# Attention with a gated feed-forward: earlier value sums, split operands for two more score steps, one split moved by a step

## The chip, the core and the metric

The kernel runs on one core of a Trainium2 chip. The core has a matrix engine (TensorE, PE in the profile; its weight loads are listed apart as PEld), VectorE (DVE), ScalarE (ACT), GpSimd (POOL) and SyncE (SP), which here does nothing but start DMA transfers. Each engine works off its own list of instructions in order, and waits where an instruction needs something that another engine or a transfer has not finished. The metric is the device time of one execution in microseconds: 544.22 us before the change, the median of three runs (544.18 to 544.31).

## The reference

The input `x` has the shape (2, 1024, 512): two sequences of 1024 tokens. What is computed, cut to its core:

```python
xn = layernorm(x)
q, k, v = (xn @ W.T + b for W, b in ((Wq, bq), (Wk, bk), (Wv, bv)))      # 32 heads of 16
att = softmax(where(causal, q @ k.T / 4, -inf));  s = (att @ v) @ Wo.T + bo
logits = xn @ W_gate.T;  w = top-2 of softmax(logits), normalized       # 8 experts of rank 16
ffn = xn @ W_base.T + b_base + sum_e w_e * (xn @ A_e.T) @ B_e.T
out = x + s * silu(ffn)
```

Everything is float32.

## The kernel before

**Units and steps.** The tokens of a sequence are cut into two chunks of 512 (`c` = 0, 1), and the 32 heads into four groups of eight (`oc`). Attention runs over 16 units `(b, oc, c)`, in the order of the list `units` (line 1387, pairs swapped at 1391): (0,0,0), (0,1,0), (0,0,1), (0,1,1), (0,2,0), (0,3,0), (0,2,1), and so on. A unit of the first chunk has 5 steps, one of the second 13; `plan` (line 1393) numbers all 144 steps. A step `n` makes the transposed scores of a stretch of keys for four pairs of heads (`scores`, line 1691), their exponentials on ScalarE, a causal mask on GpSimd (`masked`), and, one step later, the product with the values (`values`, line 1738).

**Score operands.** Heads lie in pairs within strips of 32 partitions, and a matmul takes one head of each pair (`par`). The first unit uses whole float32 operands: `qT` holds the queries twice, each time with the other head of the pair multiplied by zero (`queries(par)`, line 392), and the keys `kT` (tile kf_0_0_0) are used as they are. All later units use split operands: rounded (fp32r) values in one half of a strip and the remainder that rounding left in the other. The remainder is made by VectorE (`split_queries`, `split_keys`), the queries' copy of it by ScalarE (`copy_remainder`), and it is put into the other half of the strip by DMAs from SBUF to SBUF on SP's queue (`place_queries`, `place_keys`, two transfers each). The first unit's keys are split too, by `apart` (line 438), since the third unit, (0,0,1), attends to them; it runs at step 4 or later.

**The plan of the other work.** The order of all instructions on every engine is written out by the program itself. After each step, `fill(n)` (line 1592) places other work in this order: TensorE tasks (projections, feed-forward) as far as a share of the total and the due times ask for; splits that are due; the list `later`; zero-cost tasks such as `layernorm_task`, which have VectorE work and DMAs. An entry of `later` is a step and a function; it runs in the first `fill` that is not before the step, unless `costs` names a limit until which it may wait for ScalarE to be calm. What is placed first stays first on its engine and, for DMAs, on SP's queue. `fill(-2)` comes ahead of step 0 and holds all of `first_task` (line 362): layernorm, transposes and first projections of chunk (0,0).

**Around the change.** In `fill(0)` `early_values` (line 832) makes the first values by a scheme of seven block products instead of eight; for it VectorE first takes differences of the weights (t1 to t4, tiles wt1 to wt4) and of the tokens (s0 to s3, tiles asum). Its products p1, p2, p6, p7, p4 use two PSUM buffers in turn (`ps_mm`, `bufs=2`), so p6 starts when p1 has been added into `v`, and p4 when p6 has. p1, p2 and the first quarter of p6 stand in `fill(0)`, the rest of p6, p7 and the first quarter of p4 in `fill(1)`, the rest of p4 and the whole `qk_task` of the second unit in `fill(2)`. `layernorm_task(0, 1)` takes its statistics (four `bn_stats`) in `fill(0)`, and in `fill(1)` it normalizes, transposes half of the chunk into `sq` and calls:

```python
            if not b:
                store()
                place()
```

`store` writes `sq` to a DRAM scratch (scr<-sq), and `place` reads it back in four transfers (xnT<-scr), the first of which must wait until the write has landed. `room` counts free buffers; a task starts only when its `takes` are free. `ve` and `act` are wrappers that add up estimated time for the planner; `nc.vector` is the same engine without that.

Of the kernel before, what the change touches and what calls it, by code (L numbers as in the profile page):

```python
# [18 lines left out]
P = 128  # L19
# [12 lines left out]
NEG = -3.0e38  # L32
NF = 2 + 4 * 2 * 4
WARM = 10


Z_LOW, Z_HIGH = 1.0e-20, 1.0e20
# [60 lines left out]
def direct(ctx, tc, sound, x, wq, wk, wv, wo, wb, wa, wg, wB, bq, bk, bv, bo, bb, out):  # L98
# [148 lines left out]
    WAIT = object()  # L247
    PAUSE = object()
    turned_at, now = {}, [0]
    xns, xnTs, kTs, qTs, vs, gs, oTs, kfs = {}, {}, {}, {}, {}, {}, {}, []  # L250

    def mm_tile(name):
        return ps_mm.tile([P, D], F32, tag="mm", name=name)
# [108 lines left out]
    def first_task():  # L362

        xnT = sb.tile([P, KC, C], F32, tag="xnT", bufs=3, name="xnT_0_0")
        qT = sb.tile([P, 2, C], F32, tag="qT", bufs=2, name="qT_0_0_0")
        kT = sb.tile([P, C], F32, tag="kf", bufs=2, name="kf_0_0_0")
        xnTs[0, 0], qTs[0, 0, 0] = xnT, qT
        kfs.append(kT)
        pq = ps_av.tile([P, C], F32, tag="av", name="pq_first")
        pk = ps_av.tile([P, C], F32, tag="av", name="pk_first")  # L370

        def turn(t):
            many = KC if t else KC // 2
            for k0 in range(0, KC, many):
                pt = mm_tile("pt_x")[:, 0 : many * P]
                for k in range(many):
                    cols = slice((k0 + k) * P, (k0 + k + 1) * P)
                    nc.tensor.transpose(pt[:, k * P : (k + 1) * P], first[t][:, cols], ident)
                act.copy(
                    xnT[:, k0 : k0 + many, t * P : (t + 1) * P],  # L380
                    pt.rearrange("p (k t) -> p k t", k=many),
                )
            turned_at[0, 0] = now[0] - 5

        def project_first(ps, w, t):
            cols = slice(t * P, (t + 1) * P)
            for k in range(KC):
                nc.tensor.matmul(  # L388
                    ps[:, cols], lhsT=w[:, k, :], rhs=xnT[:, k, cols], start=k == 0, stop=k == KC - 1
                )  # L390

        def queries(par):
            ve.tensor_scalar(
                qT[:, par], pq, bq_sb[:, 0:1], half[:, par : par + 1], ALU.add, ALU.mult
            )

        def keys(t0, t1):
            cols = slice(t0 * P, t1 * P)
            act.activation(kT[:, cols], pk[:, cols], AF.Identity, bias=bk_sb[:, 0:1])

        s0 = yield from statistics(first[0 : 1])

        def halves():
            for half_ in range(2):
                normalize([first[0][:, 2 * P * half_ : 2 * P * (half_ + 1)]], *s0)

        s1 = yield from statistics(first[1:2], between=halves)
        turn(0)
        normalize(first[1:2], *s1)
        project_first(pq, wqks[0][:, 2 * KC : 3 * KC], 0)  # L410
        b_ps = mm_tile("b_ps")[:, 0 : 2 * KC]
        nc.tensor.transpose(b_ps, b_rows, ident[0 : 2 * KC, 0 : 2 * KC])
        act.copy(b_sb, b_ps)
        s2 = yield from statistics(first[2 : 3])
        turn(1)
        project_first(pk, wqks[0][:, 3 * KC :], 0)
        keys(0, 1)
        project_first(pq, wqks[0][:, 2 * KC : 3 * KC], 1)
        normalize(first[2:3], *s2)
        turn(2)  # L420
        s3 = yield from statistics(first[3 : 4])
        project_first(pk, wqks[0][:, 3 * KC :], 1)
        project_first(pq, wqks[0][:, 2 * KC : 3 * KC], 2)
        normalize(first[3:4], *s3)
        turn(3)
        room["x"] += 1
        project_first(pk, wqks[0][:, 3 * KC :], 2)
        project_first(pq, wqks[0][:, 2 * KC : 3 * KC], TT - 1)
        queries(0)
        queries(1)  # L430
        ve.stream_shuffle(b_pair, b_sb, PAIRED)
        ve.tensor_tensor(b_less, b_pair[:, 0:KC], b_pair[:, KC:], ALU.subtract)
        project_first(pk, wqks[0][:, 3 * KC :], 3)
        keys(1, TT)
        kTs[0, 0, 0] = sb.tile([P, 2, C], F32R, tag="kT", bufs=4, name="kT_0_0_0")
        low = sb.tile([P, C], F32, tag="rb", bufs=1, name="low_0_0_0")

        def apart():
            ve.stream_shuffle(low, kT, PAIRED)
            split_keys(kTs[0, 0, 0], low, low)  # L440
            later.append((now[0] + 1, lambda: place_keys(kTs[0, 0, 0], low)))

        later.append((0, lambda: pair_up(wqks[1])))
        paired = lambda: pair_up(wqks[0])
        costs[paired], costs[apart] = (1.1, 5), (1.1, 6)
        later.append((3, paired))
        later.append((4, apart))
        yield 8 * MM

    def qk_task(b, oc, c):  # L450
# [47 lines left out]
    def split_keys(kT, kf, low):  # L498

        act.activation(kT, kf.unsqueeze(1).to_broadcast([P, 2, C]), AF.Copy)  # L500
        ve.tensor_tensor(low, kf, kT[:, 0].bitcast(F32), ALU.subtract)

    def place_keys(kT, low):
        for par in range(2):
            sp.dma_start(out=kT[1 - par :: 2, par].bitcast(F32), in_=low[par::2])
# [17 lines left out]
            both = qT[:, 2 * par : 2 * par + 2].bitcast(F32)  # L523
            sp.dma_start(out=both[1 - par :: 2], in_=both[par::2])

    def last_unit(unit):
        return 1 if unit == units[-1] else 0

    def split(b, oc, c, qf, kf):

        qT, kT = split_tiles(b, oc, c)
        split_keys(kT, kf, kf)

        def queries():
            split_queries(qT, qf)
            room["acc"] += 1
            later.append((now[0] + 1, remainder))

        def remainder():
            copy_remainder(qT)  # L540
            urgent.append((now[0], lambda: place_queries(qT)))

        by = starts[b, oc, c] - last_unit((b, oc, c))
        costs[queries], costs[remainder] = (1.1, by - 4), (0.6, by - 3)
        later.append((now[0] + 1, queries))
        urgent.append((now[0] + 1, lambda: place_keys(kT, kf)))
# [282 lines left out]

    def early_values():

        x0 = xnTs[0, 0]
        at = lambda i, j: x0[:, 2 * j : 2 * j + 2, BK * i : BK * i + BK]
        early_at["w"] = raw = {
            (i, j): wv_sb[:, 2 * i : 2 * i + 2, BK * j : BK * j + BK]
            for i in range(2) for j in range(2)
        }
        t = {  # L840
            n: sb.tile([P, 2, BK], F32, tag="wp", bufs=NWP, name=f"wt{n}") for n in range(1, 5)
        }
        early_sums.update({f"t{n}": t[n] for n in t})
        early_at["s"] = s = [
            sb.tile([P, 2, BK], F32, tag=f"sum{n}", bufs=1, name=f"asum{n}") for n in range(4)
        ]
        vt = value_tile(0, 0)
        for i in range(TT):
            vs[0, i] = vt[:, i]
        hv = heads(vt)  # L850
        early_at["v"] = slot = lambda i, j: hv[:, 2 * i : 2 * i + 2, H // 2 * j : H // 2 * (j + 1), 0:HD]
        s11, s12, s21, s22 = slot(0, 0), slot(0, 1), slot(1, 0), slot(1, 1)
        ve.tensor_tensor(t[1], raw[0, 1], raw[0, 0], ALU.subtract)
        ve.tensor_tensor(s[2], at(0, 0), at(1, 0), ALU.subtract)
        ve.tensor_tensor(s[1], at(1, 1), s[2], ALU.subtract)
        ve.tensor_tensor(t[2], raw[1, 1], t[1], ALU.subtract)
        ve.tensor_tensor(t[3], raw[1, 1], raw[0, 1], ALU.subtract)
        p1 = yield from early_product("p1", at(0, 0), raw[0, 0])
        early_add(s12, p1, early_bias(0))
        ve.tensor_tensor(t[4], raw[1, 0], t[2], ALU.subtract)  # L860
# [607 lines left out]
    for b in range(NB):  # L1468
        for c in range(NC):
            s0 = starts[b, 0, c]  # L1470
            xn = [("xnT", b, c)]
            if not b and not c:
                room["x"] -= 1
                Task(1, first_task(), 8 * MM, takes={"xnT": 1, "qT": 1, "kT": 1}, uses=xn)
            else:
                Task(
                    s0 - (12 if c else 25) if b else -9, layernorm_task(b, c), 0.0, after=s0 - (44 if c == 0 else 30) if b else -9,
                    takes={"x": 1, "xnT": 1}, frees={"x": 1},
                )
# [112 lines left out]
    def fill(n):  # L1592
# [52 lines left out]
        enough = lambda more=0.65: late_by(n + 1, begins, more) > 0  # L1645
        calm = lambda more: act.free + more < begins + 0.75
        for x in [x for x in splits if x[0] <= n]:
            if room["qT"] and room["kT"] and (calm(1.1) or n >= starts[x[2]] - 5 - last_unit(x[2])):
                splits.remove(x)
                room["qT"] -= 1  # L1650
                room["kT"] -= 1
                x[1]()
# [38 lines left out]
    def scores(n):  # L1691
# [1 line left out]
        place_urgent(n)  # L1693
        ss = [ps_s.tile([P, 2, C], F32, tag="s", name=f"s{p}") for p in range(2)]
        for m, (par, kt, q0, w, col) in enumerate(pieces):
            first_unit = (b, oc, c) == units[0]
            halves = 1 if first_unit else 2
            keys = kfs[0] if first_unit else kTs[b, oc, kt // TT][:, par]
            q = qTs[b, oc, c]
            for half_ in range(halves):  # L1700
                for s in range(4):
                    rows = slice(32 * s, 32 * s + 32)


                    nc.tensor.matmul(  # L1705
                        ss[s // 2][:, s % 2, col : col + w],
                        lhsT=keys[rows, kt % TT * P : kt % TT * P + P],
                        rhs=q[rows, halves * par + half_, q0 : q0 + w],
                        start=m + half_ == 0,
                        stop=m == len(pieces) - 1 and half_ == halves - 1,  # L1710
                    )
# [572 lines left out]
```

## Time and profile before

| | us |
|---|---|
| median of the runs | 544.22 |
| the profiled execution | 544.11 |
| its span on the core | 542.3 |

Busy time of the engines in the stretches around the change, in us, from the profile:

| stretch (us) | what runs | PE | DVE | ACT | POOL |
|---|---|---|---|---|---|
| 0 to 16 | `first_task` | 14.40 | 7.40 | 4.43 | 3.12 |
| 16 to 21 | step 0, p1, p2 | 4.67 | 4.93 | 3.48 | 1.98 |
| 21 to 27 | step 1, p6, p7 | 5.90 | 5.52 | 2.05 | 1.74 |
| 27 to 33 | step 2, p4, queries of unit 2 | 6.00 | 5.97 | 2.02 | 1.80 |
| 33 to 39 | keys of unit 2, step 3 | 6.00 | 1.64 | 3.76 | 0.00 |
| 39 to 46 | steps 3 to 5 | 7.00 | 3.98 | 5.37 | 2.80 |
| 100 to 500 | most of the rest | 399.84 | 256.34 | 280.85 | 88.23 |

A row is read as the time in which the engine had an instruction at work within the stretch; what is missing to its length is idle time. TensorE is at work nearly all the time, the other engines about half of it, except for VectorE between 16 and 33 us.

### The profile page before, as it was taken

What the parts mean: (1) busy time and instruction counts of PE and PEld (TensorE: products, weight loads), DVE (VectorE), ACT (ScalarE), POOL (GpSimd) and SP (SyncE); (2) the same over time, 40 slices, a digit from 0 to 9 for tenths busy, and PEclk for the clock granted to TensorE, in tenths of its full rate; (3) what the DMA queues carried; (4) which work ended last, traced back from release to release, by engine and by line L of the source; (5) the groups of instructions that cost most, each with busy time, mean ns of one, the idle gap of its engine ahead of it and who ended that gap; (6) DMA issues with size and microseconds to landing.
All of it is one profiled execution on the core that took longest, in us unless ns stands there. A gap on an engine that the chain in (4) does not pass through costs nothing.

```text
span 542.3 us, 19668 instructions
## 1 busy us (share of the span) xinstructions
PE 532.7 (98%) x8503; PEld 280.4 (52%) x8503; DVE 340.5 (63%) x703; ACT 352.2 (65%) x390; POOL 117.0 (22%) x249
## 2 busy tenths in 40 slices
PE   8999999999999999999999999999999999999994
PEld 8546445544455554454545554454545554456661
DVE  4863586665584976566369766574176554749833
ACT  3457755777776876757667756657667776877641
POOL 2213401021033422030133321130113330121300
PEclk9999999999999999999999999999999999999998
DMA  7636356366527583813656545640134121752301
GB/s 253 157 118 201 126 171 221 95 201 203 160 100 231 186 257 123 225 42 105 196 155 199 190 131 174 199 142 24 63 98 142 61 85 46 234 176 85 100 29 59
DMA packets 67743, 78.13 MB, mean 144 GB/s; under 512 B 9928, under 2 KB 52944, under 8 KB 67136
## 3 DMA queue, kind: packets, MB, share of 16 engines
q1 hardware_dynamic: 67632, 76.78, 44.9%
q8 instruction: 69, 1.13, 0.9%
q14 instruction: 26, 0.21, 0.1%
q10 hardware_dynamic: 16, 0.00, 0.0%
HBM read 45.34 MB, written 19.37 MB: 119 GB/s over the span
## 4 chain that ended last, share of the span: by engine, by line
PE 95%; DVE 2%; ACT 1%; DMA 1%; issue 0%; SPq 0%; POOL 0%; ACTq 0%; POOLq 0%; DVEq 0%
PE av L1757 26%; PE p L258 25%; PE s L1705 18%; PE q L258 14%; PE ph L258 3%; PE po L258 2%; PE pq L258 1%; PE pk L258 1%; PE warm L213 1%; ACT pt L56 1%; PE pq_first L388 1%; PE h L258 1%; DMA kept<-w_gate 1%; PE pk_first L388 0%; DVE wt L56 0%; PE pt_o L258 0%
## 5 line engine op out<-in xcount | busy, mean ns | idle before, releaser
L56 ACT ACTIVATE pt<-s 128x1024 f32<-128x1024 f32 x288 | 290.6, 1025 | 150.8 <-PE s L1705 145.4
L1733 POOL TENSOR_SCALAR_AFFINE_SELECT pt<-pt 128x256 f32<-128x256 f32 (+1 forms) x224 | 108.3, 498 | 399.3 <-ACT pt L56 398.7
L1757 PE MATMUL av<-pt,v 128*32 128x512 f32 (+3 forms) x1680 | 154.4, 467 | 0.2 <-DVE oT L56 0.2
L1705 PE MATMUL s<-qT,kT 32*128 32x512 f32 (+3 forms) x1616 | 107.4, 363 | 0.1
L1705 PEld LDWEIGHTS s<-qT,kT 32*128 32x128 f32 x1616 | 61.5, 183 | 57.8 <-issue 34.0
L1757 PEld LDWEIGHTS av<-pt,v 128*32 128x32 f32 x1680 | 41.1, 108 | 53.5 <-issue 38.4
L258 PE MATMUL p<-wt,asum 128*32 128x256 f32 x960 | 58.4, 379 | 0.4 <-DVE v L56 0.4
L258 PE MATMUL q<-asum,wqk 128*32 128x256 f32 x832 | 51.1, 379 | 0.0
L258 PEld LDWEIGHTS p<-wt,asum 128*32 128x32 f32 x960 | 31.0, 110 | 29.9 <-issue 12.6
L258 PE MATMUL q<-xnT,wqk 128*32 128x256 f32 x624 | 39.5, 379 | 0.0
L258 PEld LDWEIGHTS q<-asum,wqk 128*32 128x32 f32 x832 | 26.8, 110 | 23.8 <-issue 6.6
L258 PEld LDWEIGHTS q<-xnT,wqk 128*32 128x32 f32 x624 | 20.2, 110 | 18.5 <-issue 6.6
L56 DVE SCALAR_TENSOR_TENSOR kf<-q,kf 128x256 f32<-128x256 f32 x39 | 16.5, 422 | 20.6 <-PE q L258 20.0
L56 DVE TENSOR_TENSOR g<-p,g 128x512 f32<-128x512 f32 x20 | 13.8, 689 | 23.5 <-PE p L258 23.4
L258 PE MATMUL p<-w,xnT 128*32 128x256 f32 x448 | 27.6, 379 | 0.0
L56 DVE TENSOR_TENSOR v<-p,v 128x512 f32<-128x512 f32 x22 | 15.0, 684 | 13.4 <-PE p L258 13.3
L258 PE MATMUL p<-w,asum 128*32 128x256 f32 x320 | 21.0, 379 | 0.0
L258 PEld LDWEIGHTS p<-w,xnT 128*32 128x32 f32 x448 | 14.9, 110 | 10.6 <-issue 3.3
L258 PEld LDWEIGHTS ph<-wag_sb,xnT 128*32 128x32 f32 x512 | 15.2, 110 | 3.9 <-issue 3.0
L56 DVE TENSOR_TENSOR x<-p,x 128x512 f32<-128x512 f32 x15 | 10.3, 685 | 10.4 <-PE p L258 10.4
L258 PE MATMUL ph<-wag_sb,xnT 128*32 128x136 f32 x512 | 16.6, 279 | 0.0
L56 ACT ACTIVATE qT<-qf 128x1024 fp32r<-128x1024 f32 x15 | 15.8, 1054 | 0.1
(153 smaller groups left out, 562.2 us busy)
## 6 DMA issues: line engine op xcount, KB each, us to landing
wt<-kept SPq DMA_DIRECT2D x36, 256.0 KB
qT<-qT SPq DMA_DIRECT2D x30, 256.0 KB
x<-in_x_dram SPq DMA_DIRECT2D x16, 256.0 KB
kept<-wqk SPq DMA_DIRECT2D x16, 256.0 KB
wqk<-kept SPq DMA_DIRECT2D x4, 1024.0 KB
kT<-kf SPq DMA_DIRECT2D x30, 128.0 KB
scr<-sq SPq DMA_DIRECT2D x6, 512.0 KB
xnT<-scr SPq DMA_DIRECT2D x24, 128.0 KB
```

Source lines behind the costliest of these rows:

```text
L56: return getattr(self.engine, name)(*args, **named)
L213: nc.tensor.matmul(warm[:, n % 4 * P : n % 4 * P + P], lhsT=ident, rhs=ident, start=True, stop=True)
L258: nc.tensor.matmul(o[j : j + 32], lhsT=lhsT[:, j : j + 32] if len(lhsT.shape) == 2 else lhsT[:, j // 32], rhs=rhs, start=start, stop=stop,)
L388: nc.tensor.matmul(ps[:, cols], lhsT=w[:, k, :], rhs=xnT[:, k, cols], start=k == 0, stop=k == KC - 1)
L1705: nc.tensor.matmul(ss[s // 2][:, s % 2, col : col + w], lhsT=keys[rows, kt % TT * P : kt % TT * P + P], rhs=q[rows, halves * par + half_, ...
L1733: nc.gpsimd.affine_select(out=d, in_=d, compare_op=ALU.is_ge, fill=0.0, base=0, pattern=[[0, d.shape[1]], [1, P]], channel_multiplier=-1,)
L1757: nc.tensor.matmul(avs_now[par][32 * s : 32 * s + 32, q0 : q0 + w], lhsT=vs[b, kt][:, h * VS - HD * par : h * VS - HD * par + HP], rhs=pt[ ...
```

## The change

- **Sums ahead.** `early_begin` is new. It takes four of the five differences that stood at the head of `early_values` (t1, t2, t3 and s2) and issues them inside `first_task`, ahead of `queries(0)`, through `nc.vector`. s1 stays where it was.
- **Split operands from step 3.** The whole `qT` and `kT` serve steps 0 to 2 only (`SPLIT_FROM = 3`). ScalarE makes the first unit's queries once more, as they are (`qf`). `apart` moves from step 4 or later to `fill(0)` without a condition; it now also shuffles and splits the queries. `remainder` and the two key transfers follow in `fill(1)`, the two query transfers in `fill(2)`, which is the last place ahead of the scores of step 3. The first task takes two `qT` buffers, and gives one back in `fill(2)`.
- **Seventh unit.** `last_unit` becomes `sooner`, and holds for (0,2,1) as well: its split may be forced at 6 instead of 5 steps ahead of its start, and the limits for its queries and its remainder come one step sooner.

```diff
+SPLIT_FROM = 3
...
-        xnTs[0, 0], qTs[0, 0, 0] = xnT, qT
-        kfs.append(kT)
+        xnTs[0, 0] = xnT
+        whole_first.extend((qT, kT))
...
         project_first(pk, wqks[0][:, 3 * KC :], 2)
+        early_begin()
         project_first(pq, wqks[0][:, 2 * KC : 3 * KC], TT - 1)
         queries(0)
         queries(1)
+        qf = sb.tile([P, C], F32, tag="qf", bufs=2, name="qf_0_0_0")
+        act.activation(qf, pq, AF.Identity, bias=bq_sb[:, 0:1])
...
         keys(1, TT)
-        kTs[0, 0, 0] = sb.tile([P, 2, C], F32R, tag="kT", bufs=4, name="kT_0_0_0")
+        q2, k2 = split_tiles(0, 0, 0)
         low = sb.tile([P, C], F32, tag="rb", bufs=1, name="low_0_0_0")
+        turns.append((SPLIT_FROM - 1, lambda: room.update(qT=room["qT"] + 1)))
 
         def apart():
+            qs = sb.tile([P, C], F32, tag="qf", bufs=2, name="qs_0_0_0")
             ve.stream_shuffle(low, kT, PAIRED)
-            split_keys(kTs[0, 0, 0], low, low)
-            later.append((now[0] + 1, lambda: place_keys(kTs[0, 0, 0], low)))
+            ve.stream_shuffle(qs, qf, PAIRED)
+            split_keys(k2, low, low)
+            split_queries(q2, qs)
+            later.append((now[0] + 1, lambda: place_keys(k2, low)))
+            later.append((now[0] + 1, remainder))
+
+        def remainder():
+            copy_remainder(q2)
+            later.append((now[0] + 1, lambda: place_queries(q2)))
 
         later.append((0, lambda: pair_up(wqks[1])))
         paired = lambda: pair_up(wqks[0])
-        costs[paired], costs[apart] = (1.1, 5), (1.1, 6)
+        costs[paired] = 1.1, 5
+        later.append((0, apart))
         later.append((3, paired))
-        later.append((4, apart))
...
-    def last_unit(unit):
-        return 1 if unit == units[-1] else 0
+    def sooner(unit):
+        return 1 if unit in (units[6], units[-1]) else 0
...
+    def early_begin():
...
+        nc.vector.tensor_tensor(t[1], raw[0, 1], raw[0, 0], ALU.subtract)
+        nc.vector.tensor_tensor(t[2], raw[1, 1], t[1], ALU.subtract)
+        nc.vector.tensor_tensor(t[3], raw[1, 1], raw[0, 1], ALU.subtract)
+        nc.vector.tensor_tensor(s[2], at(0, 0), at(1, 0), ALU.subtract)
+
+    def early_values():
...
-        ve.tensor_tensor(t[1], raw[0, 1], raw[0, 0], ALU.subtract)
-        ve.tensor_tensor(s[2], at(0, 0), at(1, 0), ALU.subtract)
         ve.tensor_tensor(s[1], at(1, 1), s[2], ALU.subtract)
-        ve.tensor_tensor(t[2], raw[1, 1], t[1], ALU.subtract)
-        ve.tensor_tensor(t[3], raw[1, 1], raw[0, 1], ALU.subtract)
...
-                Task(1, first_task(), 8 * MM, takes={"xnT": 1, "qT": 1, "kT": 1}, uses=xn)
+                Task(1, first_task(), 8 * MM, takes={"xnT": 1, "qT": 2, "kT": 1}, uses=xn)
...
-            if room["qT"] and room["kT"] and (calm(1.1) or n >= starts[x[2]] - 5 - last_unit(x[2])):
+            if room["qT"] and room["kT"] and (calm(1.1) or n >= starts[x[2]] - 5 - sooner(x[2])):
...
-            first_unit = (b, oc, c) == units[0]
-            halves = 1 if first_unit else 2
-            keys = kfs[0] if first_unit else kTs[b, oc, kt // TT][:, par]
-            q = qTs[b, oc, c]
+            whole = n < SPLIT_FROM
+            halves = 1 if whole else 2
+            keys = whole_first[1] if whole else kTs[b, oc, kt // TT][:, par]
+            q = whole_first[0] if whole else qTs[b, oc, c]
```

The tiles and slices that `early_begin` sets up (`at`, `raw`, `t`, `s`) moved into it with the four instructions, and `early_values` reads them from `early_at`.

## The prediction

> **What bounds the kernel.** I read the page's busy shares first, then its chain of waits.
>
> ```profile
> PE 532.7 (98%) x8503; PEld 280.4 (52%) x8503; DVE 340.5 (63%) x703; ACT 352.2 (65%) x390; POOL 117.0 (22%) x249
> PE 95%; DVE 2%; ACT 1%; DMA 1%; issue 0%; SPq 0%; POOL 0%; ACTq 0%; POOLq 0%; DVEq 0%
> ```
>
> TensorE is busy for 98% and carries 95% of the chain that ends last. By stretches, it misses 0.16 us between 100 and 500 us. So there is no slack after the start in which a delay could vanish: a microsecond in which TensorE stands still early is a microsecond at the end, and only less TensorE work or a closed gap gains. Next, the chain from 15 to 38 us:
>
> ```profile
> 15.08 1.47 DVE qT L56 x2
> ...
> 18.73 1.71 DVE wt L56 x2
> 20.44 0.61 DVE v L56
> 21.05 0.04 issue
> 21.10 0.64 PE p L258 x8
> ...
> 34.08 3.43 PE pk L258 x32
> 37.51 1.08 PE s L1705 x16
> ```
>
> Here VectorE bounds: its differences (`wt`, `asum`) hold up the addition of p1, and p6 waits for that addition's buffer. From 21.1 on TensorE runs unbroken up to step 3 (37.51). VectorE and SP around it, by the timeline:
>
> ```profile
> 22.16 0.41 DVE L56 TENSOR_TENSOR bv_sb<-bv_sb 128x256 f32<-128x256 f32 x1
> 22.50 0.68 DVE L56 BATCH_NORM_STATS2 st<-x 128x6 f32<-128x512 f32 x1
> ...
> 25.89 0.69 DVE L56 TENSOR_TENSOR v<-p,v 128x512 f32<-128x512 f32 x1
> ...
> 30.16 1.41 DVE L56 STREAM_TRANSPOSE sq<-x 128x256 f32<-128x256 f32 x4
> ```
>
> ```profile
> 26.63 0.16 PEld L258 LDWEIGHTS p<-wt,xnT 128*32 128x32 f32 x8 [0.29 <-DVE v L56]
> ```
>
> ```profile
> 31.60 0.33 SPq L72 DMA_DIRECT2D scr<-sq  x1
> 34.90 2.65 SPq L72 DMA_DIRECT2D xnT<-scr  x4
> 37.65 1.21 SPq L72 DMA_DIRECT2D qT<-qT  x2
> ```
>
> The reader should see two tight couplings. The addition of p6 (25.89) comes only after the four `bn_stats`, and p4 already waits for it (26.63). And SP stands still from 31.93 to 34.90 until scr<-sq has landed; what is behind xnT<-scr stands too.
>
> **Sums ahead.** Four instructions, 0.60 us from start to start (wt 16.89, asum 17.49 in the chain), go into VectorE's gap between 12.05 and 15.08, when it waits for pq_first. s2 needs the copy of the fourth tile (ACT, ends 13.75), so the four end near 14.6; cost nothing. If wv landed late the first queries would slip: 0 to 0.9 us (all of that load's traffic is over by 13.5), and I take 0. p1 can then be added at 18.9 instead of 20.36, and p6 follows p2 without the gap: chain time of p1 and p2 is 3.47 (as for the 64 matmuls at 23.80), 17.01 + 3.47 = 20.48 against 21.10, so 0.6 us gained up to there. p2's addition is bound by p2 itself (20.67), so VectorE reaches its `bn_stats` place at about 21.67 instead of 22.50.
>
> **Steps 3 and 4.** Whole: 1.08 and 1.07 us to the values (37.44 to 38.52, 41.25 to 42.32). Split, same widths: 0.72 (52.95 to 53.67) and 0.67 (62.40 to 63.07). Gain 0.36 + 0.40 = **0.76 us**.
>
> **qf.** One ACT pass of 0.69 (row qf<-pq) between 15.05 and 15.74, ahead of the keys that wait for TensorE until 15.89: hidden. Were it held until VectorE has read the same bank (16.6), the exponentials of step 0 would come 0.8 later, and still ahead of their use at 22. Zero in both cases.
>
> **apart in fill(0).** It stands ahead of `bn_stats` now. On VectorE: shuffle of the keys 21.67 to 22.41 (row 0.74), of the queries to 23.07. ScalarE rounds the keys (1.06) to 23.51, then the queries to 24.47; VectorE subtracts (0.69) from 23.54, and from 24.50 to 25.19, having waited for ScalarE. First `bn_stats` at 25.12; from there to the addition of p6 the trace has 25.89 − 22.50 = 3.39, so 28.51 to 29.20. **p4 starts at 29.24 instead of 26.63: 2.6 us late**, and TensorE stands for about 3.0 us, since it would have been there 0.6 earlier. Bounds: without any wait for ScalarE 0.85 less. ScalarE's exponentials of step 1 slip from 22.84 to 24.47; they end at 26.5, covered by that same gap. Masks on POOL follow by 27; the `rstd` behind them comes from VectorE after 28.4 anyway. The key transfers are issued near 24.3, when SP is idle (18.4 to 31.6). Taking `apart` out of its old place (47.64, 52.40, 53.49, 56.34) gains nothing: no gap of TensorE there.
>
> **The query transfers.** This is the wait that decides. Two transfers of 256 KB are new, issued in `fill(2)`; `store` and `place` of `layernorm_task` go into SP's queue in `fill(1)`, ahead of them. The data is ready early (remainder on ScalarE after the exponentials, 27.2), but SP isn't. That a ready transfer is held so shows at 46.97, where kept<-wt, whose tiles were written by 21.7, goes out on the heel of the next xnT<-scr (44.33 + 2.59). VectorE: p7's addition 29.11 instead of 26.89 (the old one had a wait of 0.31 ahead of it), so everything behind is 2.22 late and the transposes end at 33.79. From the trace's own distances: scr<-sq 33.82; + 3.30 = 37.12 xnT<-scr; + 2.75 = 39.87 query transfers. In the DMA slices the traffic of the corresponding qT<-qT (37.65) lasts to 40.65, 3.0 after its issue; at 61.53, with nothing ahead, 2.5. I take 3.0, as xnT<-scr is ahead here too: landed 42.87, **step 3 starts at 42.95**. TensorE would be there at 29.24 + (37.44 − 26.63) = 40.05, so it stands for 2.9 us more. Against 37.44 step 3 is 5.5 late.
>
> Behind step 3 nothing waits on: the second unit's transfers follow by 43.9 and land some 3 us later, its first step comes near 49.9; ScalarE and VectorE have caught up in the gap.
>
> **Seventh unit.** Its step 46 starts at 194.27; its key split ran at 176.44 in fill(40), which is the new limit already; queries (183.21) and remainder (186.65) move one step of 3.4 us ahead. No gap of TensorE lies near (0.15 of the 0.16 us between 100 and 500 lie at 118.87), ScalarE idles 0.85 ahead of the step that gets the extra 1.05, so its exponentials end 0.2 later, used 2 us later. Cost 0, at most 0.2, gain 0.
>
> **A rule against a row.** Both gaps are near the length at which TensorE's clock drops. The row: the last matmul ends at 535.18, and the granted clock falls from 1.00 to 0.50 at about 538.3 (0.80 on average from 538.0 to 538.5): 3.1 us. The Trainium skill, "TensorE: Matmul & The Clock Gate", "Why this matters for your kernels", warns of gaps over about 3 us, since an idle window takes the clock to half; its Part 1 has the window at about 3.4 us, running freely, and about as long to come back. By the rule of 3 us the first gap could cost a window at half speed: half of 3.4, 1.7 us. By the row, gaps of 3.0 and 2.9 fall short. I take none, and keep 1.7 to 2.3 for a drop (20 warm-up matmuls took 4.58 at the start, while the same shape later runs at 0.11 each: 2.3 lost).
>
> **Sum.** 5.5 − 0.76 = 4.75 us on 544.11: 548.86 for a profiled execution; the median lies 0.11 above that: **549.0 us**. The 0.6 of the sums is inside: it makes VectorE's chain earlier but adds nothing to it.
>
> **Rivals.**
> - *Faster.* The query transfers reach the tile before TensorE asks, and VectorE's load is hidden: 0.6 + 0.76 gained, 542.9. It needs both a p6 addition by 26.1 and a landing by 36.9; the landing alone decides the sign once step 3 starts later than 37.44 + 0.76 = 38.2. For it: the data is ready at 27.2, ten us ahead. Against: even unchanged xnT<-scr ends at 37.55 on SP. Chance 0.06.
> - *Only VectorE's wait.* If the query transfers don't stand behind xnT<-scr, step 3 starts at 40.05: 2.6 − 0.76 = 1.85, 546.1. For it, only that SP's order comes from the code and not from a row of the changed kernel. 0.06.
> - *A clock drop* in one of the gaps: 549.0 + 1.7 to 2.3, 550.7 to 551.3; 0.13.
> - *It doesn't do what it says*: split steps no cheaper, or gaps filled by other work that the plan brings in; about 544.2. Against: the order of tasks hangs on due times that stay. 0.03.
> - *As forecast*: 0.72, within 548.1 to 549.9.
>
> **Range.** Lower: 0.85 of ScalarE's waits and 0.5 of the landing off 549.0 give 547.6; I go to 547.4. Upper: one drop of 2.3 and 0.5 of slipped queries, 551.8. Faster or slower means by over 0.2%, about what a measurement of this kernel can tell: faster 0.06, the same 0.03, slower 0.91.
>
> **What would show it.** Right: p4's weight load waits for `DVE v` until about 29.2; SP issues qT<-qT right behind xnT<-scr near 39.9; the matmuls of step 3 begin near 43 after a gap and take 0.72; step 5 starts near 49.9 instead of 45.05; clock 1.00 throughout. Wrong: step 3 before 40, query transfers ahead of scr<-sq, `bn_stats` ahead of the shuffles, or a clock below 1.00 at 30 to 50.

## The result and the profile after

The change makes the kernel slower: 548.91 us (median of six, 548.40 to 552.08) against 544.38 for the kernel before beside it (544.18 to 544.90), a ratio of 1.0100 with a 95% interval of 1.0081 to 1.0118. The forecast was 549.0. The profiled execution took 548.40, with a span of 546.7 us; line numbers after the change are 1 higher than before up to the middle of the file, and 17 higher in `scores` and `values`.

The page of the changed kernel, busy time and the chain that ended last:

```profile
PE 533.9 (98%) x8503; PEld 281.7 (52%) x8503; DVE 342.1 (63%) x706; ACT 353.7 (65%) x393; POOL 117.4 (21%) x249
PE 96%; DVE 1%; ACT 1%; issue 0%; POOL 0%; ACTq 0%; DVEq 0%; POOLq 0%
```

The totals say almost nothing: the same 8503 matmuls, three more instructions on VectorE and three on ScalarE, and still 98%. They even hide something: TensorE is busy 1.2 us longer without having more work. The timeline of TensorE shows it, first step 2 and the values behind it before the change, then the changed kernel (start, length, the tile written, and in brackets the idle time ahead with what ended it):

```profile
27.20 1.15 PE L1705 MATMUL s<-qT,kf 32*128 32x384 f32 x16
28.28 1.07 PE L1757 MATMUL av<-pt,v 128*32 128x512 f32 x8
```

```profile
29.28 0.64 PE L259 MATMUL p<-wt,xnT 128*32 128x256 f32 x8 [3.04 <-DVE v L57]
29.85 2.02 PE L1722 MATMUL s<-qT,kf 32*128 32x384 f32 x16
...
42.92 0.80 PE L1722 MATMUL s<-qT,kT 32*128 32x384 f32 x16 [1.12 <-ACT kf L57]
46.37 0.74 PE L1722 MATMUL s<-qT,kT 32*128 32x256 f32 x16
...
49.77 0.74 PE L1722 MATMUL s<-qT,kT 32*128 32x512 f32 x8
```

Two new gaps, ahead of p4 (29.28) and of step 3 (42.92), as forecast. But between them step 2 takes 2.02 us where it took 1.15, and the values behind it (31.81) 1.82 where they took 1.07. Step 5 follows at 49.77, 4.72 later than before. By stretches (from:to, length, then busy time and instructions of PE, PEld, DVE, ACT and POOL, TensorE's granted clock, share and rate of the DMAs):

```profile
29.50:30.00 0.50, 0.50 (x12) 0.15 (x8) 0.50 (x1) 0.00 (x0) 0.24 (x1) 0.97 0.00 0
30.00:31.00 1.00, 1.00 (x8) 0.67 (x12) 0.97 (x3) 0.00 (x0) 0.00 (x0) 0.50 0.03 8
...
33.00:34.00 1.00, 1.00 (x16) 0.35 (x12) 0.91 (x3) 0.27 (x1) 0.78 (x2) 0.81 0.00 0
```

A mean of 0.97 over 29.5 to 30.0 puts the fall of the clock at 29.97, a mean of 0.81 over 33 to 34 its return at 33.38: 3.41 us at half speed. The forecast had a clock of 1.00 throughout. VectorE and SP, on the other hand, do what it said:

```profile
25.14 0.69 DVE L57 BATCH_NORM_STATS2 st<-x 128x6 f32<-128x512 f32 x1
...
28.54 1.48 DVE L57 TENSOR_TENSOR v<-p,v 128x512 f32<-128x512 f32 x2
```

```profile
33.94 0.34 SPq L73 DMA_DIRECT2D scr<-sq  x1
36.61 2.65 SPq L73 DMA_DIRECT2D xnT<-scr  x4
39.36 3.37 SPq L73 DMA_DIRECT2D qT<-qT  x4
```

The addition of p6 comes 2.65 later than before, behind the two shuffles, two differences and four `bn_stats`; the query transfers leave right behind xnT<-scr.

One wait bears a wrong name. Step 3 is put down to `ACT kf`, which ended at 42.56, 0.36 ahead of it, and it does not read that tile, which holds the second unit's keys. In q_early below step 3 begins at 41.79 without a wait, ahead of that same instruction (41.94); in after_warm_both the same wait reads `DMA qT<-qT`. So step 3 waits for the transfers.

### The profile page after: what moved, and what is told of

Read it like the earlier page. It is cut to its first block, busy times and chain, and to the rows that moved or that the text cites. A ratio compares the mean times of both kernels' runs of the same rounds, so it can differ in the third digit from the quotient of the medians.

```text
span 546.7 us, 19683 instructions
## 1 busy us (share of the span) xinstructions
PE 533.9 (98%) x8503; PEld 281.7 (52%) x8503; DVE 342.1 (63%) x706; ACT 353.7 (65%) x393; POOL 117.4 (21%) x249
## 4 chain that ended last, share of the span: by engine, by line
PE 96%; DVE 1%; ACT 1%; issue 0%; POOL 0%; ACTq 0%; DVEq 0%; POOLq 0%
PE av L1774 26%; PE p L259 26%; PE s L1722 19%; PE q L259 14%; PE ph L259 3%; PE po L259 2%; PE pk L259 1%; PE pq L259 1%; PE warm L214 1%; ACT pt L57 1%; PE pq_first L389 1%; PE h L259 1%; PE pk_first L389 1%; DVE st L57 0%; PE pt_o L259 0%
## 5 line engine op out<-in xcount | busy, mean ns | idle before, releaser
L1722 PE MATMUL s<-qT,kT 32*128 32x512 f32 (+3 forms) x1648 | 108.9, 362 | 1.2 <-ACT kf L57 1.1
L1722 PEld LDWEIGHTS s<-qT,kT 32*128 32x128 f32 x1648 | 62.7, 183 | 59.6 <-issue 32.8
L57 DVE TENSOR_TENSOR qT<-qf,qT 128x512 fp32r<-128x512 f32 x15 | 10.3, 685 | 15.9 <-ACT qT L57 15.8
L259 PE MATMUL p<-wt,xnT 128*32 128x256 f32 x224 | 14.6, 379 | 3.0 <-DVE v L57 3.0
```

What stands on the lines that cost most here:

```text
L57: return getattr(self.engine, name)(*args, **named)
L259: nc.tensor.matmul(o[j : j + 32], lhsT=lhsT[:, j : j + 32] if len(lhsT.shape) == 2 else lhsT[:, j // 32], rhs=rhs, start=start, stop=stop,)
L1722: nc.tensor.matmul(ss[s // 2][:, s % 2, col : col + w], lhsT=keys[rows, kt % TT * P : kt % TT * P + P], rhs=q[rows, halves * par + half_, ...
```

## The experiments

Whole-kernel times can't be compared by spans alone, since the time ahead of the first scores differs by up to 0.6 us between profiled executions (15.87 to 16.43). The last column is therefore what each trace has from the start of the first scores to the start of the last product (po), less the 517.36 of the kernel before (15.94 to 533.30). The ratio is to runs of the kernel before on the same chip beside it (medians 544.09 to 544.38). The trace is of one execution of each kernel; the medians are of 4 to 21 runs.

| kernel | median us | ratio, 95% interval | trace, us |
|---|---|---|---|
| the change | 548.91 | 1.0100 (1.0081, 1.0118) | +4.73 |
| sums_only | 543.38 | 0.9984 (0.9977, 0.9991) | -0.68 |
| split_only | 549.31 | 1.0092 (1.0077, 1.0108) | +5.20 |
| seventh_only | 544.39 | 1.0006 (0.9997, 1.0015) | +0.14 |
| q_early | 547.75 | 1.0055 (1.0040, 1.0071) | +4.31 |
| q_early_warm | 548.75 | 1.0082 (1.0066, 1.0097) | +4.62 |
| q_early_warm12 | 546.60 | 1.0045 (1.0029, 1.0061) | +2.62 |
| hidden | 543.26 | 0.9984 (0.9978, 0.9991) | -0.82 |
| hidden_q_late | 549.22 | 1.0096 (1.0080, 1.0112) | +4.82 |
| hidden2 | 543.17 | 0.9979 (0.9972, 0.9987) | -0.99 |
| after_warm12 | 550.40 | 1.0118 (1.0102, 1.0133) | +6.52 |
| after_warm_both | 549.00 | 1.0098 (1.0074, 1.0122) | +4.85 |
| after_again | 549.23 | 1.0083 (1.0068, 1.0099) | +9.89 |

### The three parts alone

sums_only is the kernel before with `early_begin` and nothing else of the change:

```diff
         project_first(pk, wqks[0][:, 3 * KC :], 2)
+        early_begin()
         project_first(pq, wqks[0][:, 2 * KC : 3 * KC], TT - 1)
```

> Only the four differences ahead, on the kernel before; every other instruction keeps its place. My theory: the differences cost nothing where they go and close the gap ahead of p6, 0.6 us: ratio 0.9989, about 543.8. p4 starts about 26.1 and waits for nothing or for at most 0.1. Rival (the early differences delay the first queries or add nothing): 544.4 or above, first scores later than 15.94.

split_only is the change with the four differences back at the head of `early_values`:

```diff
-        early_begin()
         project_first(pq, wqks[0][:, 2 * KC : 3 * KC], TT - 1)
...
+        ve.tensor_tensor(t[1], raw[0, 1], raw[0, 0], ALU.subtract)
+        ve.tensor_tensor(s[2], at(0, 0), at(1, 0), ALU.subtract)
         ve.tensor_tensor(s[1], at(1, 1), s[2], ALU.subtract)
+        ve.tensor_tensor(t[2], raw[1, 1], t[1], ALU.subtract)
+        ve.tensor_tensor(t[3], raw[1, 1], raw[0, 1], ALU.subtract)
```

> The change without the four differences ahead: split operands from step 3 and the seventh unit's split stay. My theory (two waits, VectorE's chain and SP's queue): VectorE reaches its statistics 0.83 later, p4 starts near 30.1, SP sends the query transfers near 40.2, step 3 starts near 43.75, 0.83 later than with the change: about 549.7. Rival (TensorE's clock drop sets the time): anything between 548 and 552, by how long the clock stays low. Rival (the early differences are what costs): 544 to 546.

seventh_only is the kernel before with the longer limit for the seventh unit:

```diff
     def last_unit(unit):
-        return 1 if unit == units[-1] else 0
+        return 1 if unit in (units[6], units[-1]) else 0
```

> Only the seventh unit's split one step sooner, on the kernel before. My theory: no wait of TensorE is there, so 544.26 within 0.2. Rival (the earlier split pushes ScalarE's exponentials or SP's transfers of steps 41 to 46): up to 1 us slower.

The sums gain 0.9 us by the medians, a little over the expectation; the trace has 0.68. The first scores of that execution begin at 16.35, later than 15.94, but the sums are not the reason: in the change, which has them too, they begin at 15.99, and in split_only, which has not, at 16.20. In the timeline of TensorE of sums_only the wait ahead of p6 is gone (p6 starts at 20.90, on the heel of p2), and so is the 0.29 ahead of p4:

```profile
26.42 0.62 PE L258 MATMUL p<-wt,xnT 128*32 128x256 f32 x8
```

split_only waits 3.23 ahead of p4 and begins step 3 at 43.68, where 43.75 was expected. So the loss is in the split operands of steps 3 and 4, and the sums only work against it.

The seventh unit gains nothing, and its traces show a small loss. TensorE's steps 45 and 46, first before the change, then in seventh_only:

```profile
190.86 0.75 PE L1705 MATMUL s<-qT,kT 32*128 32x256 f32 x16
...
194.27 0.74 PE L1705 MATMUL s<-qT,kT 32*128 32x512 f32 x8
```

```profile
190.77 0.75 PE L1705 MATMUL s<-qT,kT 32*128 32x256 f32 x16
...
194.48 0.74 PE L1705 MATMUL s<-qT,kT 32*128 32x512 f32 x8
```

From one to the next it takes 3.71 us instead of 3.41, and step 46 begins 0.2 later; 0.14 of that is left at the end. The same 3.71 stands in hidden and hidden2 below, 3.73 in the change. The medians are too coarse for it (1.0006, with an interval that holds 1).

### VectorE's wait or the transfers

q_early sends the query transfers one `fill` sooner, ahead of scr<-sq:

```diff
         def remainder():
             copy_remainder(q2)
-            later.append((now[0] + 1, lambda: place_queries(q2)))
+            place_queries(q2)
```

> The change with the first unit's query transfers issued in fill(1), ahead of scr<-sq on SP. Theory that SP's order sets step 3: the wait for the transfers goes, step 3 starts when TensorE arrives. With the clock drop of the changed kernel's profile still there (p4 still waits until 29.28) that is 41.9, 1.05 earlier: 547.9; without a drop 40.1: 546.1. Rival (step 3 waits for ScalarE's kf, as the trace has it): step 3 still 0.3 behind the end of kf, 548.9.

q_early_warm adds 22 idle matmuls behind p7, into a score buffer, with a result that nothing reads, so that the clock can't drop while TensorE waits; q_early_warm12 does it with 12:

```diff
         p7 = yield from early_product("p7", s[2], t[3])
+        warm2 = ps_s.tile([P, 2, C], F32, tag="s", name="warm2")
+        for n in range(12):
+            nc.tensor.matmul(warm2[:, 0, 0:P], lhsT=ident, rhs=ident, start=True, stop=True)
         early_add(s21, p7, s12)
```

> As the kernel with the early query transfers, and 22 idle matmuls of 128 columns between p7 and p4, so that TensorE is at work in most of the gap of 3.0 us; p4 can't start earlier for that. If the gap drops the clock and the drop costs: the clock stays at 1.00, step 3 starts at 40.1, 546.1, 1.7 faster than without the idle matmuls. If the drop costs nothing: the same time as without them.

> As the kernel with early query transfers, with 12 instead of 22 idle matmuls in the gap ahead of p4. They took 0.236 each there, so 12 take 2.8 and end ahead of p4's start at 29.3. If the clock drop is what the runs of 548.4 to 548.7 of that kernel had and those of 546.9 to 547.1 had not: all runs near 546.5 to 547.0, granted clock 0.997 or above. If not: 547 to 548.7 again.

q_early has its transfers out at 26.94, seven us ahead of scr<-sq (34.01), by SP's timeline, and step 3 no longer waits (TensorE's timeline):

```profile
26.94 1.11 SPq L73 DMA_DIRECT2D qT<-qT  x2
```

```profile
41.79 0.80 PE L1722 MATMUL s<-qT,kT 32*128 32x384 f32 x16
```

Its four times fall into two pairs: 546.86 and 547.09 with mean granted clocks of 0.998 and 0.998, 548.41 and 548.71 with 0.994 and 0.993; the median of 547.75 lies between the pairs. The profiled execution is one of the second pair and has the clock at half from 30.02 to 33.4, after a gap of 3.04 us. That the same gap did not drop it in the first pair is read from their mean clocks alone; after_again below has a gap of 3.04 without a drop in a trace. q_early_warm was mis-sized: each of these float32 matmuls stands in the trace as two passes (so the 20 warm-up matmuls that the prediction reads off the start are ten, `WARM = 10`), the 44 passes took 5.18 us, and p4 started at 31.16 instead of 29.4; it cost by work what it saved in clock, and decides nothing beyond its clock of 1.00. q_early_warm12 is the clean one: 24 passes take 2.95 us, and the clock stays at 1.00 from 20 to 60:

```profile
29.47 0.64 PE L259 MATMUL p<-wt,xnT 128*32 128x256 f32 x8 [0.16 <-DVE v L57]
...
40.28 0.80 PE L1725 MATMUL s<-qT,kT 32*128 32x384 f32 x16
```

p4 starts where VectorE lets it, 2.58 later than before (each counted from its first scores), step 3 waits for nothing, and the time is 546.60. **With VectorE's wait as the only one left, the change costs 2.5 to 2.6 us** (546.60 less the 544.09 beside it, and the trace); what the sums and the split steps gain is already taken off.

hidden takes the other wait away. The shuffles go into VectorE's idle time ahead of the addition of p1, the roundings stay in `fill(0)` on ScalarE, `qf` is made behind the keys, the two differences move to `fill(1)`, behind the additions of p6 and p7, and the query transfers follow at once:

```diff
+        ve.stream_shuffle(low, kT, PAIRED)
+        ve.stream_shuffle(qs, qf, PAIRED)
...
+        def rounded():
+            act.activation(k2, low.unsqueeze(1).to_broadcast([P, 2, C]), AF.Copy)
+            high = q2.rearrange("p (a h) c -> p a h c", a=2)[:, :, 0]
+            act.activation(high, qs.unsqueeze(1).to_broadcast([P, 2, C]), AF.Copy)
...
         def apart():
-            ve.stream_shuffle(low, kT, PAIRED)
-            ve.stream_shuffle(qs, qf, PAIRED)
-            split_keys(k2, low, low)
-            split_queries(q2, qs)
...
+            ve.tensor_tensor(low, low, k2[:, 0].bitcast(F32), ALU.subtract)
+            ve.tensor_tensor(q2[:, 1], qs, q2[:, 0].bitcast(F32), ALU.subtract)
             copy_remainder(q2)
+            place_keys(k2, low)
+            place_queries(q2)
...
-        later.append((0, apart))
+        later.append((0, rounded))
+        later.append((1, apart))
```

> A rearranged change: sums ahead; both shuffles go into VectorE's free time ahead of the addition of p1; ScalarE's two roundings into fill(0); the two subtractions, the remainder and all four transfers into fill(1), behind p7's addition on VectorE and ahead of scr<-sq on SP. If the two waits are all that the change costs, p4 starts near 26.1 and step 3 near 36.9 without a wait, and the gains stay: 0.6 + 0.76 = 1.36, about 542.9. If split steps or the sums cost something else: 544 or more.

hidden_q_late is hidden with the query transfers back in `fill(2)`, where the change has them:

```diff
             place_keys(k2, low)
-            place_queries(q2)
+            later.append((now[0] + 1, lambda: place_queries(q2)))
```

> The rearranged change, but the query transfers are issued in fill(2), behind xnT<-scr, as in the change. Only SP's order is left as a cost. p4 near 26.1 as there; transposes end near 32.2, transfers are sent near 38.0 and land near 41.0, so step 3 starts 3.6 later than before the change: 544.26 + 3.6 - 0.76 = 547.1. If the gap of 4.1 us ahead of step 3 lowers the clock for a window, 1.7 more: 548.8. Rival (a query transfer in fill(2) is early enough by itself): 542.9.

hidden is 543.26, 0.8 us below the kernel before: with both waits gone the loss is gone. But this is no more than the sums bring alone (sums_only 0.9984, hidden 0.9984, nearly the same interval); what the split steps add is taken up below. hidden_q_late shows the transfers by themselves. TensorE's timeline, then SP's:

```profile
25.95 0.62 PE L259 MATMUL p<-wt,xnT 128*32 128x256 f32 x8
...
41.02 0.79 PE L1725 MATMUL s<-qT,kT 32*128 32x384 f32 x16 [4.22 <-issue]
41.74 1.69 PE L1777 MATMUL av<-pt,v 128*32 128x384 f32 x16
```

```profile
34.69 2.65 SPq L73 DMA_DIRECT2D xnT<-scr  x4
37.44 2.48 SPq L73 DMA_DIRECT2D qT<-qT  x4
```

p4 is not held (25.95), yet step 3 starts at 41.02, as expected to a tenth, and the values behind it take 1.69 instead of 1.07, since the clock is at half from 42.06 to 45.47. 549.22 is the upper of the two values expected (548.8, with a drop). **One line, the place of two DMA instructions on SP's queue, is worth 6 us** between these two kernels: 4.2 of standing still and 1.7 of clock.

### What the clock costs

The change drops the clock in its first gap, and its time is still that of a forecast without any drop. Three runs bear on that. after_warm12 is the change with the 12 idle matmuls ahead of p4. after_warm_both also fills the second gap, with ten idle matmuls into the score tile that step 3 overwrites:

```diff
         ss = [ps_s.tile([P, 2, C], F32, tag="s", name=f"s{p}") for p in range(2)]
+        for _ in range(10 if n == 3 else 0):
+            nc.tensor.matmul(ss[0][:, 0, 0:P], lhsT=ident, rhs=ident, start=True, stop=True)
```

after_again is the change itself once more, without an edit.

> The change plus 12 idle matmuls on TensorE ahead of p4, in the time in which it waits for VectorE, so that the clock stays at 1.00 there. If the half-speed stretch cost nothing since it lay inside the wait for the query transfers: 548.9 as the change, step 3 still at about 42.9, after a gap of about 2.8 instead of 1.1 (which may drop the clock in its turn: up to 1.7 more). If the drop is part of what the change costs: 547.2.

> The change with both gaps of TensorE filled with idle matmuls: 12 ahead of p4, 10 ahead of step 3, so that the clock stays at 1.00 from 20 to 60. If after_warm12's 1.5 over the change is the half-speed stretch that it has from 43.9 to 47.3, and not the idle matmuls: 548.9, as the change, with step 3 at about 43 and its two steps at 0.72 and 0.67. If the idle matmuls themselves cost it: 550.4, as after_warm12.

> The change once more, to see whether the two times near 552 of its first six come back: 548.4 to 549.1 if they do not.

after_warm12 came out slower than the change: 550.40. TensorE's timeline and two stretches of it:

```profile
43.24 0.80 PE L1725 MATMUL s<-qT,kT 32*128 32x384 f32 x16 [2.94 <-issue]
43.96 1.94 PE L1777 MATMUL av<-pt,v 128*32 128x384 f32 x16
```

```profile
43.50:44.00 0.50, 0.50 (x20) 0.43 (x17) 0.50 (x3) 0.00 (x0) 0.00 (x0) 0.94 0.26 98
...
47.00:47.50 0.50, 0.50 (x12) 0.27 (x8) 0.00 (x0) 0.01 (x1) 0.42 (x2) 0.65 0.00 0
```

With the first drop gone TensorE reaches step 3 earlier, stands for 2.94 us instead of 1.12, and the clock falls there, from 43.94 to 47.35, when nothing is waiting any more. Filling that gap too brings it back to 549.00, with a clock of 1.00 throughout (TensorE's timeline of after_warm_both):

```profile
43.46 0.79 PE L1727 MATMUL s<-qT,kT 32*128 32x384 f32 x16 [0.54 <-DMA qT<-qT]
```

So a half-speed stretch of 3.41 us costs 1.7 us by the traces (6.52 less 4.85) where TensorE is the bound; by the medians it is 1.2 (6.09 and 4.85 over the kernel before beside each), from four runs each, with intervals that overlap. Where it ends in a wait it costs nothing: the change, with a drop, has +4.73, and after_warm_both, without one, +4.85. In the change the drop ate into the wait for the transfers.

after_again gave 548.50, 548.85, 549.23, and 551.67 and 554.45. The last one was profiled; SP's timeline, then TensorE's, then two stretches:

```profile
34.37 0.34 SPq L73 DMA_DIRECT2D scr<-sq  x1
39.10 2.65 SPq L73 DMA_DIRECT2D xnT<-scr  x4
```

```profile
29.71 0.64 PE L259 MATMUL p<-wt,xnT 128*32 128x256 f32 x8 [3.04 <-DVE v L57]
...
45.50 1.33 PE L1722 MATMUL s<-qT,kT 32*128 32x384 f32 x16 [4.91 <-issue]
```

```profile
45.00:45.50 0.50, 0.00 (x1) 0.03 (x2) 0.00 (x0) 0.00 (x0) 0.00 (x0) 0.52 1.07 426
...
51.50:52.00 0.50, 0.50 (x12) 0.03 (x4) 0.00 (x0) 0.00 (x0) 0.00 (x0) 0.66 0.77 228
```

The first gap, 3.04 long as in the change, did not drop the clock here (step 2, at 30.28, takes 1.15). scr<-sq took 4.73 us to land instead of 2.67, so step 3 waited 4.91; then the clock was at half from 45.02 to 51.84, twice 3.41. That accounts for the longer time: 2.06 for the landing and 3.41 for 6.82 us at half speed, less 0.24 for the 0.48 in which TensorE stood anyway, 5.2 against the 5.16 between +9.89 and +4.73. Why the write landed late stays open, and so do the other executions between 551.0 and 552.1 (three of the change's eleven, one each of after_warm12 and after_warm_both), none of which was profiled. The one of after_warm_both has a mean clock of 0.995 beside 0.996 in its others, so a drop of the clock is not what made it longer.

### What the split steps are worth

hidden was expected at 542.9, with the 0.76 of steps 3 and 4. hidden2 changes one condition in `qk_task`, for the keys of the second unit: ScalarE rounds them straight from PSUM and VectorE makes `kf`, so that ScalarE has one instruction less ahead of the exponentials of step 3:

```diff
-        if c:
+        if c or oc == 1:
```

> hidden (p6's add and both query transfers early, p4 unheld) with the second unit's keys rounded by ScalarE straight from PSUM and kf made by VectorE, so that ScalarE is free for step 3's exps about 0.56 us sooner and step 4 need not wait for them. If ScalarE's order is what gives back the 0.7 of the split steps: step 5 about 0.3 sooner than in hidden (44.2 instead of 44.55), 542.9. If step 4 is bound by something else: 543.26, as hidden.

TensorE's steps 3 to 5 before the change and step 5 of sums_only; then TensorE's timeline of hidden and ScalarE's; below them the same two of hidden2:

```profile
37.44 1.15 PE L1705 MATMUL s<-qT,kf 32*128 32x384 f32 x16
41.25 1.15 PE L1705 MATMUL s<-qT,kf 32*128 32x256 f32 x16
45.05 0.74 PE L1705 MATMUL s<-qT,kT 32*128 32x512 f32 x8
```

```profile
44.81 0.74 PE L1710 MATMUL s<-qT,kT 32*128 32x512 f32 x8
```

```profile
37.23 0.80 PE L1725 MATMUL s<-qT,kT 32*128 32x384 f32 x16
40.68 1.07 PE L1725 MATMUL s<-qT,kT 32*128 32x256 f32 x16
44.55 0.74 PE L1725 MATMUL s<-qT,kT 32*128 32x512 f32 x8
```

```profile
38.08 1.06 ACT L57 ACTIVATE kT<-kf 128x1024 fp32r<-128x1024 f32 x1
39.04 1.92 ACT L57 ACTIVATE pt<-s 128x1024 f32<-128x1024 f32 x2
```

```profile
36.99 0.79 PE L1725 MATMUL s<-qT,kT 32*128 32x384 f32 x16
40.44 0.74 PE L1725 MATMUL s<-qT,kT 32*128 32x256 f32 x16
43.86 0.74 PE L1725 MATMUL s<-qT,kT 32*128 32x512 f32 x8
```

```profile
37.13 1.11 ACT L57 ACTIVATE kT<-pk,b_pair 128x1024 fp32r<-128x1024 f32 x1 [0.27 <-PE pk L259]
38.14 1.93 ACT L57 ACTIVATE pt<-s 128x1024 f32<-128x1024 f32 x2
```

In hidden step 4 takes 1.07 although it is split: it waits for the exponentials of step 3, whose second half ends at 40.96. From step 3 to step 5 the kernel before has 7.61 us (37.44 to 45.05), hidden 7.32, hidden2 6.87. So with ScalarE's old order the split steps bring 0.29 us, and with the new one 0.74, nearly the 0.76 of the forecast.

Little of that reaches the end. Counted from the first scores, step 5 begins at 28.46 in sums_only, at 28.18 in hidden and at 27.72 in hidden2, so hidden is ahead of sums_only by 0.28 and hidden2 by 0.74, and both keep this up to step 44. By step 46 about 0.17 of it is gone in both, at the place where seventh_only loses its 0.2; sums_only has not that part of the change. At 529 hidden2 waits 0.49 for ScalarE's oT, the other two 0.21, which takes 0.28 more from it. At the last product 0.14 and 0.31 are left (-0.82 and -0.99 against -0.68). The medians do not show even this: sums_only, hidden and hidden2 have overlapping intervals, all below 1. So hidden2, at 543.17, has the lowest median, but neither it nor hidden is shown to be faster than the sums alone.

## Why the prediction held, and where it did not

- **The sums.** Forecast to end near 14.6 with p1 added at 18.9 and p6 0.6 earlier: 14.61, 19.07, and 20.54 instead of 21.10. Alone they bring 0.7 to 0.9.
- **qf.** The bound was right and the taken side wrong: ScalarE began it at 16.75 instead of 15.05, 0.09 after VectorE's second reading of the same tile had ended (16.66), the exponentials of step 0 began at 17.80 instead of about 17.1, and as said it cost nothing.
- **apart ahead of `bn_stats`.** 25.12, 28.51 and 29.24 were forecast for the first `bn_stats`, the addition of p6 and p4; 25.14, 28.54 and 29.28 measured.
- **The query transfers.** The order on SP was right, and the two sizes were not: scr<-sq took 2.67 us to the issue of xnT<-scr, not 3.30, and the transfers needed 3.56 from their issue to step 3, not 3.1. That 42.92 came out against 42.95 is luck, since the two errors nearly cancel. The 3.30 was one draw from a wide scatter: in the fourteen traces this write takes 2.63 to 2.70 in six, 2.93 to 3.85 in seven and 4.73 in after_again. A range of 0.5 for the landing was too narrow.
- **The clock: the step that failed.** "By the row, gaps of 3.0 and 2.9 fall short. I take none." The gap of 3.04 drops it in the change, and the second gap, 2.94 once the first drop no longer shortens it, drops it in after_warm12. The 3.1 us of the row at the end of before were taken for a threshold, and they were one instance of a time that differs from execution to execution: in the fourteen traces the clock falls 2.4 us (q_early) to 5.4 us (the change, split_only) after the last matmul of the kernel. In the change it fell 3.73 us after TensorE's last matmul, 0.69 after it had begun again. A length of gap as a rule does no better, since 3.04 in after_again did not drop it; the forecast gave a drop 0.13, and both profiled executions of the change have one. That the forecast time came out all the same is luck: the first drop fell where the second wait swallowed it, and shortened that gap to 1.12. Without it the second gap drops the clock, and the rival with a drop (550.7 to 551.3) is near the 550.40 that after_warm12 shows.
- **Steps 3 and 4.** 0.72 and 0.67 to the values were forecast, 0.73 (42.92 to 43.65) and 0.68 (46.37 to 47.05) measured. But the gain belongs to this schedule: the "Faster" rival took 0.76 along to 542.9, and where both waits are gone ScalarE binds step 4, which leaves 0.29 of the 0.76 and 543.26. The same holds for the rival "Only VectorE's wait": 546.1 forecast, 546.60 measured in q_early_warm12.
- **Seventh unit.** 0 forecast, at most 0.2. The bound held; the traces have 0.14 to 0.2, since step 46 comes 0.2 late. In seventh_only a weight load of the values behind step 45 waits 0.18 for GpSimd's mask, and four masks take 2.42 us there instead of 2.22; VectorE's order beside them has changed too. What makes the mask late is left open.
- **The sum.** 4.75 forecast for the profiled execution, 4.73 in the trace up to the last product; the whole of the profiled execution took 548.40, 4.29 more than the one before, and the medians differ by 4.5 (548.91 and 544.38).

What is *shown*: either wait alone makes the kernel slower (q_early_warm12, hidden_q_late); with both gone it is faster than before (hidden), by about what the sums bring alone; and the transfers are late by their place on SP's queue. What is *not shown* is a gain of the split steps in the time of the whole kernel. What is only *argued*: the split of the 4.73 into VectorE's and SP's shares, since the transfers themselves are late in part because VectorE is (step 3 at 41.02 in hidden_q_late, 42.92 in the change).

## What to carry to other kernels

Before moving a step ahead, list every queue that its instructions enter and what stands at the head of each: here two ready DMAs stood behind one that waited for a write to DRAM, and their place was worth 6 us, with the clock drop that the wait brought. A gap of TensorE costs its length, and one near 3 us can cost about 1.7 more for the clock (it did after 2.94, and did not in one execution with 3.04), unless another wait follows that swallows the loss; so of two gaps, filling only the first can make a kernel slower. A gain on the bounding engine is kept only until the next engine in the loop binds; look at its order of instructions before booking it. And a kernel that is faster after several edits says nothing about each of them: here hidden looks like proof for the split steps until it is put beside the sums alone.

## What the runs showed of the hardware

- **The clock fits fixed windows of 3.41 us, and not a length of gap.** Every drop before the end of a kernel lasted 3.41 us or twice that. In the window of 3.41 that ends with the fall TensorE was busy for 0.56 us (split_only, fall at 30.67), 0.66 (q_early, 30.02), 0.69 (the change, 29.97), 0.70 (after_warm12, 43.94) and 1.04 (hidden_q_late, 42.06), which is 16% to 30%, and not at all in after_again (45.02). Windows counted back further on the same grid, after which the clock stayed at 1.00, were busier: 62% and 49% in after_again (24.55 to 27.96 and 27.96 to 31.37, with the gap of 3.04 in them), 46% in hidden_q_late, and 40% at the end of split_only. Two of these windows, in hidden_q_late with a fall at its end and in split_only without:

```profile
38.65:42.06 3.41, 1.04 (x20) 0.84 (x24) 2.03 (x5) 0.15 (x1) 0.00 (x0) 1.00 1.04 371
```

```profile
539.26:542.67 3.41, 1.38 (x16) 0.28 (x8) 2.46 (x4) 0.00 (x0) 1.26 (x1) 1.00 0.03 7
```

If such windows are what decides, the share of work below which one drops the clock lies between 30% and 40% in these traces; that is an estimate from these few cases. The Trainium skill, "TensorE: Matmul & The Clock Gate", "What's actually happening", has a free-running window of 3413 ns, which agrees; its table asks for an idle window, and "HAM oscillation" for gaps over about 3.4 us, where these runs show drops after gaps of 2.94 and 3.04 in windows that were not idle to the end.
- **The return took a busier window once.** In after_again, after 4.91 us of idleness, the clock came back only after 6.82: TensorE had been busy for 2.93 of the first 3.41 us, 86%, and for all of the next. In the other cases the first window at half speed was full, and the clock came back at its end.
- **A write to DRAM of 512 KB took 2.63 to 4.73 us** (scr<-sq, from its issue to that of the read that waits for it, the first of each of the fourteen traces), and the change itself has 2.67 in one execution and 4.73 in another; so the time of a kernel that hangs on it scatters by 2 us.
